# Cross-attention's keys and values by seven block products, made between self-attention's steps and handed on through DRAM

## The chip, the cores and the metric

The kernel runs on one core of a Trainium2 chip, with no work on the other cores. The metric is the device time of one execution in microseconds; the comparison uses the median of several executions. Its engines are called here by these names: PE is TensorE (matrix products and transposes, with results in PSUM), PEld is its weight load, DVE is VectorE, ACT is ScalarE, POOL is GpSimd and SP is SyncE, which issues most of the transfers between DRAM and SBUF. Each engine works through its own queue in order.

## The reference

One layer of a decoder in f32, on 8 sequences of 256 tokens with 1024 features, followed by a memory block and a last normalization:

```python
x = _layernorm(x + attn(x))              # 32 heads of 32, 8 key heads, causal
x = _layernorm(x + xattn(x, ctx))        # 32 heads of 128, 8 key heads
...                                      # memory block, sum, last normalization

# in xattn:
q = (query @ Wq).reshape(nb, q_len, H, D).transpose(0, 2, 1, 3)
k = (key @ Wk).reshape(nb, q_len, KVH, D).transpose(0, 2, 1, 3)
v = (value @ Wv).reshape(nb, q_len, KVH, D).transpose(0, 2, 1, 3)
q = q * cos + _rotate_half(q) * sin
k = k * cos + _rotate_half(k) * sin
k = jnp.repeat(k, GROUPS, axis=1)
v = jnp.repeat(v, GROUPS, axis=1)
scores = jnp.einsum('bhqd,bhkd->bhqk', q, k) / jnp.sqrt(jnp.float32(D))
scores = jnp.where(mask == 0, jnp.float32(-1000000000.0), scores)
attn = jax.nn.softmax(scores, axis=-1)
x = jnp.einsum('bhqk,bhkd->bhqd', attn, v)
return x.transpose(0, 2, 1, 3).reshape(nb, q_len, H * D) @ Wo
```

`key` and `value` are both the context `ctx`, 8 x 256 x 1024. Nothing in the keys and values of cross-attention depends on self-attention. The positions, and so the tables of cosines and sines, come from an input and are the same for queries and keys.

## The kernel before

Self-attention and cross-attention run one after the other.

**Self-attention** (L137 to L465) is a loop over 64 steps `s`, eight for each sequence `b`; step `c` of a sequence handles four heads. In a step TensorE transposes the four attention tiles (`transposed`, L280), does some other work (`others`, L357), projects the query of step s + 3 (`query`, L231), forms the weighted sum (`weighted`, L292) and makes the scores of step s + 2 (`scores`, L238). The other work is an output projection of the last sequence (`project_out`, L321) where c < 4, and a projection of the next sequence's keys or values where c is 4 or more; in steps 5 and 6 the normalized rows of the last sequence are also turned and written to DRAM for cross-attention (`turn`, L340). `scores` issues eight maxima on VectorE (L262), eight exponentials on ScalarE (L267) and four scalings on GpSimd (L274). The copy of a transposed tile out of PSUM (L289) is on VectorE for heads 0 and 2, on ScalarE for heads 1 and 3. The rotation of a projected query (`rope`, L200) takes a copy on ScalarE, one product on GpSimd (L202) and three operations on VectorE, the last of which (L207) needs GpSimd's product.

**Seven products.** Cross-attention's queries and output projection are already formed by a scheme with seven block products in place of eight: `xa_query` (L590) splits a pair of query heads, 256 output columns, and a quarter of the tokens, 512, into 2 x 2 blocks and adds the seven products `p1` to `p7` up in PSUM copies. It needs sums of weight blocks, made once: `sum_queries` and `sum_outputs` (L382, L397) load two weight tiles, combine them by four operations on GpSimd (`combine`, L380) and write the results to DRAM. Thirty-two of these sums are spread over self-attention's steps. It also needs sums of the input's blocks, T1 to T4, which `load_x1T` (L484) makes for each quarter.

**Cross-attention** (L834) runs over four quarters of 512 tokens (two sequences each) and 32 heads `H`; four heads share a key head `G`. While head H is transposed and weighted, the scores of head H + 1 are made. Between them stand the query parts, the output parts of the last group, and the next group's keys and values. These are plain products: `xa_keys` (L566) multiplies 8 tiles of weights with the context, 512 tokens wide, in one PSUM bank, and rotates the result; `xa_values` (L571) multiplies each 128-token chunk of the context with the value weights, 128 wide. The keys and values of a group live in SBUF, two of each. The last group of a quarter also loads the next quarter's context, positions and mask, and turns its tables (`xa_tables`, L538). Where there is room, `next_fill` (L828) puts in parts of the memory block.

**What sets the order.** TensorE's order is the program's order, by hand (L92). On the other engines the planner of the framework places the instructions by readiness, and of those that are ready the one earlier in the program first; it also assigns the buffers. A pool with n buffers makes the allocation n + 1 wait for a release. Weights of all kinds, and the turned rows, share seven buffers `w4` (L101) and are loaded by SP. PSUM has eight banks: in self-attention two `mm`, two `tr` and four for scores; in cross-attention four `mm`, two `tr`, two for scores. All transposes go through `tr`. `self.xa_early` (L469) loads quarter 0's inputs four steps before the end of self-attention, into space that self-attention's keys, values and inputs have freed.

Of the kernel before, what the change touches and what calls it, by code (L numbers as in the profile page):

```python
# [29 lines left out]
SA_STEPS = B * KC  # L30

# [10 lines left out]
W4 = 7  # L42
# [5 lines left out]
@with_exitstack  # L48
def decoder_layer(ctx: ExitStack, tc: tile.TileContext, a, out: bass.AP):

    Layer(ctx, tc, a, out).run()


class Layer:
    def __init__(self, ctx, tc, a, out):
# [5 lines left out]
        self.p_mm = [self.pool("mm", 2, space=PSUM)]  # L74
        self.turns = 0
        self.p_tr = self.pool("tr", 2, space=PSUM)
# [6 lines left out]
    def run(self):  # L83
# [7 lines left out]
        self.bias = self.const.tile([P, NB * 2, S], F32, name="bias")  # L91
# [17 lines left out]
    def tr(self):  # L109
        return self.p_tr.tile([P, 512], F32, name="tr")  # L110
# [26 lines left out]
    def self_attention(self):  # L137
# [50 lines left out]
        def project(lhs, xT):  # L188
# [7 lines left out]
            raw = uni.tile([P, S], F32, name="raw", bufs=2)  # L196
# [3 lines left out]
        def rope(dst, raw):  # L200
# [3 lines left out]
            t2 = uni.tile([P, S], F32, name="t2", bufs=2)  # L204
# [6 lines left out]
        def keys(b, i):  # L211
            if i == 0:
                kTs[b] = uni.tile([P, 2, S], F32, name="kT", bufs=2)
                vs[b] = uni.tile([P, 2, SA_KV * SA_D], F32, name="v", bufs=2)
            rope(kTs[b][:, i, :], project(wk[:, :, i * P : (i + 1) * P], xTs[b]))
# [15 lines left out]
        def query(s):  # L231
# [3 lines left out]
            qTs[s] = uni.tile([P, S], F32, name="qT", bufs=3)  # L235
            rope(qTs[s], raw)

        def scores(s):  # L238
# [15 lines left out]
            for sc in scs:  # L254
                att = sp.tile([P, 2, 384], F32, name="att", bufs=6)
# [24 lines left out]
        def transposed(s, j):  # L280
# [7 lines left out]
            at = sp.tile([P, 384], F32, name="at", bufs=6)  # L288
# [24 lines left out]
        def load_out(b, half):  # L313
            cols = slice(half * 512, (half + 1) * 512)
            wos[b, half] = []
            for c in range(0, KC, 2):
                w = sp.tile([P, 2, 512], F32, name="sa_wo", bufs=5)
# [22 lines left out]
        def turn(b, tt):  # L340
# [3 lines left out]
            for j in range(2):  # L344
                ps = self.tr()
# [11 lines left out]
        def others(s):  # L357
# [13 lines left out]
            elif c > 4:  # L371
                parts.append([lambda: self.xa_tables(0), lambda: self.xa_keys(0), lambda: self.xa_values(0, range(QT))][c - 5])
# [4 lines left out]
        self.query_sums, self.out_sums = {}, {}  # L377

# [3 lines left out]
        def sum_queries(m):  # L382

            wa = self.weights([P, KC, XA_D], a["xa_wq"][2 * m])
            wb = self.weights([P, KC, XA_D], a["xa_wq"][2 * m + 1])
            a11, a12, a21, a22 = wa[:, :4, :], wa[:, 4:, :], wb[:, :4, :], wb[:, 4:, :]
            combine(ALU.add, a22, a21, a22)
            combine(ALU.subtract, a21, a11, a21)
            combine(ALU.subtract, a11, a22, a11)
            combine(ALU.subtract, a12, a12, a11)  # L390
            self.query_sums[m] = []
            for i, w in enumerate((wa, wb)):
                d = self.dram.tile([P, KC, XA_D], F32, name=f"qs{i}_{m}")
                nc.gpsimd.dma_start(out=d, in_=w)
                self.query_sums[m].append(d)

        def sum_outputs(g, u):  # L397

            if u == 0:
                self.out_sums[g] = [self.dram.tile([P, 2, 512], F32, name=f"ot{i}_{g}") for i in range(4)]  # L400
            wa = self.weights([P, 2, 512], a["xa_wo"][GRP * g + u].rearrange("p (k c) -> p k c", k=2))
            wb = self.weights([P, 2, 512], a["xa_wo"][GRP * g + 2 + u].rearrange("p (k c) -> p k c", k=2))
            b11, b12, b21, b22 = wa[:, 0, :], wa[:, 1, :], wb[:, 0, :], wb[:, 1, :]
            combine(ALU.subtract, b11, b12, b11)
            combine(ALU.subtract, b12, b22, b12)
            combine(ALU.subtract, b22, b22, b11)
            combine(ALU.subtract, b21, b21, b22)
            for i, w in enumerate((b11, b22, b12, b21)):
                nc.gpsimd.dma_start(out=self.out_sums[g][i][:, u, :], in_=w)

        sums = [lambda m=m: sum_queries(m) for m in range(QP)]
        sums += [lambda g=g, u=u: sum_outputs(g, u) for g in range(XA_KV) for u in range(2)]

# [15 lines left out]
        for s in range(last):  # L429
# [9 lines left out]
            if s + 3 < last:  # L439
                query(s + 3)  # L440
# [871 lines left out]
```

## Time and profile before

| What | Value |
|---|---|
| Median of 3 executions | 3740.25 us (3739.35 to 3741.8) |
| The profiled execution | 3738.25 us, span of the profile 3736.5 us |
| Mean granted clock of TensorE | 0.978 |
| Busy shares | PE 96%, PEld 68%, DVE 50%, ACT 25%, POOL 25% |
| Moved by DMA | 494.39 MB, mean 132 GB/s |
| Chain that ended last | PE 87%, POOL 4%, DMA 3% |
| L600, query products, 128x256, x3584 | 841.5 us busy, 380 ns each |
| L561, keys, 128x512, x512 | 225.0 us busy, 592 ns each |
| L580, values, 128x128, x2048 | 238.8 us busy, 275 ns each |
| L380, sums of weights on POOL, x128 | 164.9 us busy |

A busy time of a group is the union of its instructions; the mean of one instruction includes the time that it takes to drain, so it is longer than the distance from one start to the next. The 40 slices are equal parts of the span, 93.4 us each; a digit is the busy share in tenths, and in the row of the clock the granted clock in tenths. Self-attention lies in the first ten slices, its last weighted sum ends at 926.83 us.

| Stretch | PE busy | DVE busy | POOL busy | granted clock | GB/s |
|---|---|---|---|---|---|
| 20 to 60 us | 31.32 of 40 | 16.99 | 18.48 | 0.88 | 266 |
| 240 to 400 us | 142.40 of 160 | 73.32 | 93.73 | 0.95 | 200 |
| 400 to 600 us | 180.78 of 200 | 100.23 | 120.64 | 0.96 | 206 |
| 600 to 800 us | 176.54 of 200 | 101.90 | 115.30 | 0.96 | 181 |
| 1100 to 1700 us | 599.51 of 600 | 306.91 | 101.59 | 1.00 | 117 |
| 3000 to 3600 us | 597.70 of 600 | 303.31 | 89.90 | 1.00 | 106 |

### The profile page before, as it was taken

Reading aid. Unit: us, or ns where it says so; the run is one execution under the profiler, and the core shown is the slowest. Engines: PE = TensorE matmul, PEld = TensorE weight load, DVE = VectorE, ACT = ScalarE, POOL = GpSimd, SP = SyncE. Lnnn points to the kernel's source line nnn. Section 1 sums busy time; section 2 is a strip of 40 time slices with the busy share of each in tenths; the row PEclk is TensorE's granted clock in tenths of the full one; section 3 lists DMA queues with packets and bytes.
Section 4 is the critical chain, followed back from the end, with each engine's and each line's share of the span. In section 5 each row is a group of like instructions: output and inputs, shape, how many; then the busy total and the mean of one; then the engine's idle time right before and its main releaser. Section 6 shows DMA issues by size and latency. Waiting matters only on the chain.

```text
span 3736.5 us, 47734 instructions
## 1 busy us (share of the span) xinstructions
PE 3595.0 (96%) x17294; PEld 2559.4 (68%) x17294; DVE 1851.0 (50%) x5574; ACT 942.0 (25%) x2920; POOL 933.9 (25%) x971
## 2 busy tenths in 40 slices
PE   7889988898999999999999999999999999999997
PEld 5656655665777777677777777777777777777764
DVE  3445544545444444564444555544455464444467
ACT  2333433333122212212121221222222121222213
POOL 4565556663111111121111111111112121111110
PEclk8999999999999999999999999999999999999996
DMA  6365555555433333433233343333334332333323
GB/s 229 119 241 179 198 180 191 203 202 173 150 99 108 107 104 110 161 122 107 94 109 103 105 158 102 126 106 102 99 103 152 113 121 98 101 103 105 103 81 129
DMA packets 182298, 494.39 MB, mean 132 GB/s; under 512 B 17072, under 2 KB 45040, under 8 KB 180144
## 3 DMA queue, kind: packets, MB, share of 16 engines
q1 hardware_dynamic: 142592, 406.73, 32.9%
q0 software_dynamic: 15104, 52.44, 3.8%
q10 hardware_dynamic: 24368, 32.18, 2.3%
q8 instruction: 138, 2.26, 0.3%
q14 instruction: 96, 0.79, 0.1%
HBM read 425.88 MB, written 65.40 MB: 131 GB/s over the span
## 4 chain that ended last, share of the span: by engine, by line
PE 87%; POOL 4%; DMA 3%; ACT 2%; DVE 2%; issue 1%; SPq 0%; POOLq 0%; DVEq 0%; ACTq 0%
PE mm L600 21%; PE mm L764 20%; PE mm L580 6%; PE mm L192 6%; PE sc L665 6%; PE mm L561 6%; PE mm L715 6%; PE mm L329 4%; PE tr L699 3%; POOL w L380 2%; ACT att L267 2%; PE tr L284 2%; PE mm L1013 2%; PE mm L1149 1%; DMA w<-in_xa_wq 1%
## 5 line engine op out<-in xcount | busy, mean ns | idle before, releaser
L600 PE MATMUL mm<-x1T,w 128*128 128x256 f32 x3584 | 841.5, 380 | 3.2 <-DVE res L771 3.2
L600 PEld LDWEIGHTS mm<-x1T,w 128*128 128x128 f32 x3584 | 668.7, 190 | 129.0 <-issue 44.8
L556 POOL TENSOR_TENSOR qT<-qT,t 128x512 f32<-128x512 f32 x128 | 162.3, 1268 | 1334.2 <-DVE t L555 1161.8
L764 PE MATMUL mm<-w,xoS 128*128 128x512 f32 x992 | 446.2, 592 | 1.4 <-DVE t L555 1.4
L679 ACT ACTIVATE xatt<-xatt,nmax 128x256 f32<-128x256 f32 x512 | 255.7, 500 | 691.9 <-DVE nmax L674 679.1
L764 PE MATMUL mm<-w,xoT 128*128 128x512 f32 x744 | 334.4, 592 | 0.0
L764 PEld LDWEIGHTS mm<-w,xoS 128*128 128x128 f32 x992 | 188.2, 190 | 186.8 <-issue 172.7
L267 ACT ACTIVATE att<-att,nmax 128x128 f32<-128x128 f32 (+1 forms) x512 | 225.4, 442 | 249.0 <-DVE nmax L262 249.0
L771 DVE TENSOR_TENSOR acc<-mm,acc 128x512 f32<-128x512 f32 x216 | 148.5, 689 | 275.2 <-PE mm L764 275.1
L665 PE MATMUL sc<-kT,qT 128*128 128x256 f32 x1024 | 263.7, 381 | 0.0
L192 PE MATMUL mm<-xT,w 128*128 128x256 f32 x1024 | 258.4, 410 | 0.0
L607 DVE TENSOR_TENSOR raw<-mm,half 128x256 f32<-128x256 f32 x256 | 107.8, 421 | 298.7 <-PE mm L600 298.6
L274 POOL TENSOR_TENSOR att<-att,rec 128x256 f32<-128x256 f32 (+1 forms) x256 | 205.9, 827 | 156.0 <-DVE rec L271 149.6
L715 PE MATMUL mm<-xat,v 128*128 128x256 f32 x1024 | 243.3, 380 | 0.9 <-ACT xat L704 0.9
L580 PEld LDWEIGHTS mm<-w,ctxT 128*128 128x128 f32 x2048 | 238.5, 192 | 3.2
L580 PE MATMUL mm<-w,ctxT 128*128 128x128 f32 x2048 | 238.8, 275 | 0.0
L764 PEld LDWEIGHTS mm<-w,xoT 128*128 128x128 f32 x744 | 141.4, 190 | 138.7 <-issue 114.6
L192 PEld LDWEIGHTS mm<-xT,w 128*128 128x128 f32 x1024 | 210.1, 211 | 31.3
L730 POOL TENSOR_TENSOR xoS<-xoT 128x512 f32<-128x512 f32 x62 | 78.5, 1265 | 603.9 <-ACT xoT L724 603.9
L561 PE MATMUL mm<-ctxT,w 128*128 128x512 f32 x512 | 225.0, 592 | 1.4 <-DMA w<-in_xa_wk 1.4
L329 PE MATMUL mm<-sa_wo,sa_oT 128*128 128x512 f32 x512 | 225.0, 592 | 0.0
L771 DVE TENSOR_TENSOR res<-mm,res 128x512 f32<-128x512 f32 x186 | 127.9, 687 | 193.2 <-PE mm L764 170.8
(187 smaller groups left out, 4710.5 us busy)
## 6 DMA issues: line engine op xcount, KB each, us to landing
w<-in_xa_wo SPq DMA_DIRECT2D x129, 512.0 KB, 3.8
w<-qs SPq DMA_DIRECT2D x128, 512.0 KB, 3.3
w<-ot SPq DMA_DIRECT2D x124, 512.0 KB, 3.3
w<-in_xa_wq SPq DMA_DIRECT2D x96, 512.0 KB, 3.5
w<-in_sa_wq SPq DMA_DIRECT2D x64, 512.0 KB, 5.6
sa_wo<-in_sa_wo SPq DMA_DIRECT2D x64, 512.0 KB, 4.6
qs<-w POOLq DMA_DIRECT2D x32, 512.0 KB, 4.0
ot<-w POOLq DMA_DIRECT2D x64, 256.0 KB, 4.0
```

Source lines behind the costliest of these rows:

```text
L192: nc.tensor.matmul(ps[:, :S], lhsT=lhs[:, k, :], rhs=xT[:, k, :], start=(k == 0), stop=(k == KC - 1),)
L267: nc.scalar.activation(att[:, jj, lo:hi], att[:, jj, lo:hi], AF.Exp, bias=nmax[:, i : i + 1], scale=-1.0, accum_out=sums[:, i : i + 1],)
L274: nc.gpsimd.tensor_tensor(att[:, :, lo:hi], att[:, :, lo:hi], rec[:, :, i : i + 1].to_broadcast([P, 2, hi - lo]), ALU.mult,)
L329: nc.tensor.matmul(ps, lhsT=oTs[b * KC + c][:, tt * P : (tt + 1) * P], rhs=wos[b, half][c // 2][:, c % 2, :], start=(c == 0), stop=(c == K ...
L561: self.nc.tensor.matmul(ps, lhsT=w[:, k, :], rhs=rhs(k), start=(k == 0), stop=(k == KC - 1))
L580: nc.tensor.matmul(ps[:, tt * P : (tt + 1) * P], lhsT=self.ctxT[:, k, tt * P : (tt + 1) * P], rhs=self.wv[:, k, :], start=(k == 0), stop=( ...
L600: nc.tensor.matmul(ps[:, :S], lhsT=lhs[:, k, :], rhs=self.xb[q][rhs][:, k, :], start=(k == 0), stop=(k == 3),)
L665: nc.tensor.matmul(sc[:, qt, :], lhsT=qT[:, q0 : q0 + P], rhs=kT[:, b * S : (b + 1) * S], start=True, stop=True,)
L679: nc.scalar.activation(att[:, qt, :], att[:, qt, :], AF.Exp, bias=nmax[:, qt : qt + 1], scale=-1.0, accum_out=sums[:, qt : qt + 1],)
L715: nc.tensor.matmul(po[:, b * S : (b + 1) * S], lhsT=self.v[G][:, NB * b + kt, :], rhs=at[:, kt * S : (kt + 1) * S], start=(kt == 0), stop= ...
L764: nc.tensor.matmul(ps, lhsT=oT[lhs][:, u, off + p * P : off + (p + 1) * P], rhs=w[:, u, :], start=(u == 0), stop=(u == 1),)
L771: nc.vector.tensor_tensor(dst, ps, dst, ALU.add)
```

## The change

- `xa_query`'s seven products become a function `seven` for any pair of weights. Cross-attention's keys and values go through it too (`xa_keys_values`): for each quarter and pair of key heads seven products for the keys, 256 wide, and seven for the values in a turned form, where the context is the stationary operand and the weights move, 128 wide.
- These 224 products, four per step, are made in self-attention's steps 4 to 59. Rotated keys, values and the tables of each quarter go to DRAM and are loaded by cross-attention, keys and values one group ahead.
- The context is loaded in blocks with their sums, once per quarter, in self-attention (`xa_context`). The weights of keys and values get their own sums, eight more; every sum is loaded in one step and combined in the next.
- Self-attention's step is reordered: scores of step s + 1 first, then the transposes one at a time with products, the query of s + 2 and the other work between them. Scores are now one step ahead, queries two.
- Buffers: weights nine instead of seven; attention and transposed tiles of self-attention four instead of six; its output weights four instead of five. PSUM: three `mm` and one `tr` in self-attention, four and two in cross-attention. Several tiles of self-attention move from a shared pool to its own.
- In cross-attention the keys and values go away, the two blocks of a head are transposed one at a time with a query part between, and filler has two places per head.

```diff
-W4 = 7
+W4 = 9
+KV_BEGIN, KV_END = 4, 60
...
-        self.p_mm = [self.pool("mm", 2, space=PSUM)]
-        self.p_tr = self.pool("tr", 2, space=PSUM)
+        self.p_mm = [self.pool("mm", 3, space=PSUM)] * 3
+        self.p_tr = [self.pool("tr", 1, space=PSUM)]
...
-                att = sp.tile([P, 2, 384], F32, name="att", bufs=6)
+                att = sp.tile([P, 2, 384], F32, name="att", bufs=4)
-            at = sp.tile([P, 384], F32, name="at", bufs=6)
+            at = sp.tile([P, 384], F32, name="at", bufs=4)
-                w = sp.tile([P, 2, 512], F32, name="sa_wo", bufs=5)
+                w = sp.tile([P, 2, 512], F32, name="sa_wo", bufs=4)
...
+        def sums_of_inputs(name, m):
+            wa = self.weights([P, KC, XA_D], a[name][2 * m])
+            wb = self.weights([P, KC, XA_D], a[name][2 * m + 1])
+            def run():
...
+            return run
...
+        sums = [lambda n=n, m=m: sums_of_inputs(n, m) for m in range(XA_KV // 2) for n in ("xa_wk", "xa_wv")]
+        sums += [lambda m=m: sums_of_inputs("xa_wq", m) for m in range(QP)]
+        sums += [lambda g=g, u=u: sums_of_outputs(g, u) for g in range(XA_KV) for u in range(2)]
...
+        products = [part for q in range(NQ) for m in range(XA_KV // 2) for part in self.xa_keys_values(q, m)]
...
-            ats = [transposed(s, 0), transposed(s, 1)]
-            for part in others(s):
-                part()
-            ats += [transposed(s, 2), transposed(s, 3)]
-            if s + 3 < last:
-                query(s + 3)
-            if s >= 3 and (s - 3) * len(sums) // 56 < (s - 2) * len(sums) // 56 <= len(sums):
-                sums[(s - 3) * len(sums) // 56]()
-            weighted(s, ats)
-            if s + 2 < last:
-                scores(s + 2)
+            done = later
+            later = begins[s]() if s in begins else None
+            n = NQ * XA_KV // 2 * 14 // (KV_END - KV_BEGIN)
...
+            first = (s - KV_BEGIN) * n % (XA_KV // 2 * 14) == 0
...
+            if s + 1 < last:
+                scores(s + 1)
+            ats = [transposed(s, 0)]
+            if not first:
+                one()
+            ats.append(transposed(s, 1))
+            if not first:
+                one()
+            if done:
+                done()
+            ats.append(transposed(s, 2))
+            if s + 2 < last:
+                query(s + 2)
+            ats.append(transposed(s, 3))
+            for part in others(s):
+                part()
+            weighted(s, ats)
+            while mine:
+                one()
...
+    def seven(self, name, m, xb, turned, done):
...
+        def product(w, block):
+            ps = self.mm()
+            rhs = xb()[block]
+            if turned:
+                for t in range(2):
+                    for k in range(4):
+                        nc.tensor.matmul(
+                            ps[:, t * P : (t + 1) * P], lhsT=rhs[:, k, t * P : (t + 1) * P], rhs=w[:, k, :],
+                            start=(k == 0), stop=(k == 3),
+                        )
+            else:
+                for k in range(4):
+                    nc.tensor.matmul(
+                        ps[:, :S], lhsT=w[:, k, :], rhs=rhs[:, k, :], start=(k == 0), stop=(k == 3)
+                    )
...
+    def xa_keys_values(self, q, m):
+        def keys(i, c):
+            G = q * XA_KV + 2 * m + i
+            kT = self.hp.tile([P, TQ], F32, name="kx", bufs=2)
+            self.xa_rope(kT, c)
+            self.kT_d[G] = self.dram.tile([P, TQ], F32, name=f"kT_{G}")
+            nc.gpsimd.dma_start(out=self.kT_d[G], in_=kT)
+        def values(i, c):
...
+            nc.gpsimd.dma_start(out=self.v_d[G], in_=c.rearrange("p (t d) -> p t d", d=XA_D))
...
             for i, dst in enumerate((self.cos, self.sin)):
-                nc.vector.tensor_copy(dst[:, tt * P : (tt + 1) * P], ps[:, i * P : (i + 1) * P])
+                (nc.scalar.copy if i else nc.vector.tensor_copy)(
+                    dst[:, tt * P : (tt + 1) * P], ps[:, i * P : (i + 1) * P]
+                )
+        self.tables_d[q] = self.dram.tile([P, 2, TQ], F32, name=f"tables_{q}")
...
             out()
-            self.xa_transposed(H)
+            self.xa_transposed(H, 0)
             if not waits:
                 query()
...
-            elif i == 0:
-                self.xa_keys(G + 1)
-            else:
-                self.xa_values(G + 1, range(2 * i - 2, 2 * i))
+            self.xa_transposed(H, 1)
...
+            self.next_fill()
             self.xa_weighted(H)
```

## The prediction

> **What bounds the kernel now.** I read the busy shares and the 40 slices first, then TensorE's own waits, then two stretches of the timeline.
>
> ```profile
> PE   7889988898999999999999999999999999999997
> DVE  3445544545444444564444555544455464444467
> PEclk8999999999999999999999999999999999999996
> ```
>
> TensorE is full from the eleventh slice on (93.4 us each) and not before it. Self-attention fills the first ten slices. No other engine comes near full. So in cross-attention only fewer or cheaper TensorE instructions help; in self-attention it is the waits.
>
> How much is lost there? In the timeline a step without a gap, from the scores at 510.60 us to those at 524.04, takes 13.44 us, 6.87 of it an output projection (16 matmuls); the bare step is 6.57, and a key or value projection adds 3.46. The 64 bare steps (420.5), 28 output projections (192.4), 28 projections for the next sequence (96.9), 14 turns at 0.95 (13.3), quarter 0's tables, keys and values (1.0 + 6.97 + 7.14), less 12.3 done before the loop, plus 25.9 in front of it, make 752 us. From the first projection at 10.51 to the last weighted sum at 926.83 are 916.3 us. So **164 us are lost**, 28 of them up to the end of step 3 at 91.14, where four bare steps take 51.6.
>
> ```profile
> PE tr L284 <- DVE at L289: 61.8, 17, 9.7
> PE tr L284 <- ACT at L289: 21.4, 32, 0.9
> ...
> DVE qT L207 <- POOL t L202: 79.3, 17, 12.1
> ...
> POOL w L380 <- DMA w<-in_xa_wo: 18.1, 10, 5.0
> POOL w L380 <- DMA w<-in_xa_wq: 17.1, 6, 8.1
> ```
>
> These are lines of the waits (total, times, longest): TensorE's over the whole run, the others in 100 to 900 us. TensorE waits at the attention's transposes for their PSUM bank. The rotation of queries waits on GpSimd, which stands in line at weight sums whose operands have not landed. One step shows the first wait:
>
> ```profile
> 432.69 0.94 PE L247 MATMUL sc<-kT,qT 32*128 32x128 f32 x16
> 433.55 0.88 PE L284 MATMUL tr<-ident,att 128*128 128x128 f32 x6
> 434.02 0.28 DVE L262 CUSTOM_DVE_ANT_0 att<-sc,mask 128x128 f32<-128x128 f32 x1
> 436.34 0.53 DVE L289 COPY at<-tr 128x384 f32<-128x384 f32 x1
> 437.87 0.46 ACT L289 COPY at<-tr 128x384 f32<-128x384 f32 x1
> ```
>
> The transposes are over at 434.4, yet VectorE copies the first one only at 436.34, behind all eight max operations of the scores that stand earlier in the program; ScalarE copies the second behind all eight exponentials. From the first max operation the copies end after 2.85 and 4.3 us. The step from 457.49 and that from 510.60 show the same distances.
>
> **The products: 55 us saved.**
>
> ```profile
> 1302.58 3.60 PE L764 MATMUL mm<-w,xoS 128*128 128x512 f32 x8
> 1306.01 1.04 PE L699 MATMUL tr<-ident,xatt 128*128 128x128 f32 x8
> 1306.88 1.89 PE L600 MATMUL mm<-x1T,w 128*128 128x256 f32 x8
> 1308.61 3.73 PE L580 MATMUL mm<-w,ctxT 128*128 128x128 f32 x32
> 1312.18 1.89 PE L715 MATMUL mm<-xat,v 128*128 128x256 f32 x8
> ```
>
> Start to start (each busy time holds a drain that overlaps the next line): eight instructions 512 wide take 3.43 us, eight 256 wide 1.73, 32 of 128 wide 3.57. One matmul in the code is two instructions here. Now: keys 32 x 6.87 = 219.8, values 64 x 3.57 = 228.5, together 448.3. After: four quarters, four pairs of heads, seven products make 112 for keys at 1.73 = 193.8, and 112 for values (two column halves, four chunks each, 128 wide) at 1.785 = 199.9, together 393.7. Saved: **54.6**.
>
> A rule speaks against this. The Trainium skill, "TensorE: Matmul & The Clock Gate", section "Back-to-back issue gap", gives streams of loads and matmuls 81 ns at width 128 and 131 ns at 512: narrow matmuls cost more per column. A line through both gives about 98 ns at 256, 1.5 times the price per column, so keys would cost 7/8 x 219.8 x 1.5 = 288 instead of 194 and the saving would become a loss of 40. The rows show 0.429 us at 512 and 0.216 at 256, the same per column within 1%, for these f32 tiles. I take the rows.
>
> **What self-attention loses afterwards: 146 us.** Four products per step, 7 us, stand in steps 4 to 59. A step becomes 20.4 us (output projection) or 17.0 (others) of TensorE work. The softmax chain, which now holds short steps at 12 to 13, is then covered. But the transposes keep one bank instead of two. With the scores at time 0, they end at 0.86, the first transpose at 1.22, a product at 2.95. The second transpose needs the copy of the first: VectorE starts on the max operations at about 1.1 (in cross-attention, 1.07 after the scores' start at 1320.80) and the copy ends at 3.95, TensorE goes on at 4.1. That is 1.15 us, and I take 1.35, because the last product's addition (0.42) or a key rotation (2.06) can stand ahead. The third transpose, at 6.2 or later, finds ScalarE's copy done (5.4). Bounds: 0 where the copy slips ahead of the max operations, 2.9 where a rotation always stands ahead. In the sum:
> - 48 plain steps: 65.
> - Four steps in which a new quarter's context begins, with no product between transposes: 2.8 + 0.9 = 3.7 each, 15.
> - Start and steps 0 to 3, as now less a little: 28.
> - Last four steps, two without products, and the first block loads behind the freed space: 16 (8 to 30).
> - Tables: eight transposes per quarter, between the first transpose and its copy, sharing its bank: 3 each, 12 (4 to 25).
> - Differences of the context blocks (three VectorE operations of 2.06 per quarter) and late weights: 10 (0 to 40).
>
> So the waits change from 164 to 146: **18 us** come back. Gaps near 1 us leave the clock alone: 513 to 526 us, with none, was granted 1.00; 474 to 487, around a gap of 3.3, 0.75.
>
> **Edits that I cost at nothing, and their cover.**
> - VectorE: 14 additions at 0.42 per pair, 94 us, beside 66 of rotations that move along. It was busy 450 of the first 950 us and stays near half; TensorE's products cover it. Uncovered, it delays the copies above.
> - GpSimd: eight more sums (32 operations of 1.29, 16 stores of 0.57: 50 us), 31 more rotation adds (39), 64 stores of keys and values (36), three more block differences and 12 gathers (19). 520 us in the first 950, issues included, become 665 of some 1290. A store of values waits for VectorE's addition, and the scaling of attention and the queries' first rotation product stand behind it: at most 0.42 each, against 6 us between that product and the scores that need it.
> - Sums are loaded one step before they are combined, 17 us against 3.8 to landing. That removes GpSimd's 35 us at L380; what then comes last is the bank above.
> - SP's queue: 172 MB in 20 to 950 us become 275, 215 GB/s; 436 to 448 us ran at 325. Stores of tables wait for their copies with weight loads behind them; nine slots, with some five loads per step, give more than a step of lead. Four output weight tiles instead of five: the next half's loads wait for a projection, a step ahead of their use, against 4.6 us to land.
> - Renamed tiles issue nothing. Four attention tiles suffice, as the scores now come one step ahead at the step's start instead of two at its end.
> - Cross-attention loads keys and values (256 KB each) three heads before use. Its bank counts stay. Without filler, the weighted sum follows the second transpose at once: ScalarE's copy comes out 0.25 + 0.53 later, the first block's matmuls cover 0.86. I take 0.1 for some 90 heads, **10 us** (0 to 40). Filler twice per head has work enough between dependent parts.
>
> **Sum:** 3738.25 - 54.6 - 18 + 10 = 3675 against the profiled execution (span 3736.5). The median is 2 us above it: **3677**.
>
> **Rivals.**
> 1. *The bank wait is hidden* (copies run early): 65 us go, 3612. For it: a planner places VectorE's work. Against: in every step that I looked at the copy came behind the eight. Chance 0.22.
> 2. *GpSimd's queue still stands at the sums*: slower. Now 17 rotations wait for it, and around 480.68 it costs TensorE a 3.3 us gap and a query projection at half clock (5.8 for 3.6), 5.5 together. Sums rise from 32 to 40, and their loads wait for slots that earlier sums hold; SP already shows that:
>
> ```profile
> SPq L102 <- DMA ot<-w: 109.4, 28, 12.4
> SPq L102 <- DMA qs<-w: 97.7, 23, 7.6
> ```
>
> With 14 such steps left of the present 17 the time is 3677 + 77 = 3754; it decides from 12 on. Against: the load has a step's lead. Chance 0.17, and 0.06 for a few such steps, near no change.
> 3. *The forecast*: the bank wait replaces the others, 3677, chance 0.55.
>
> That the products don't fall to seven eighths is excluded by the code's counts.
>
> **Numbers.** Case 1 and the forecast are faster: 0.77. A change within 0.2% (7.5 us, about what can be told from none) has 0.06, slower 0.17. The range runs from case 1 to case 2, 3605 to 3755; the forecast's own is 3640 to 3715.
>
> **What would show it.** 896 key instructions 256 wide at 0.216 and 1792 of values 128 wide at 0.112 start to start; self-attention ending near 1290 us; TensorE's largest wait at the attention's transposes for VectorE's copy, about 50 times 1.3 us; no half-clock slices between 100 and 1200; L380's wait for loads near zero. I am wrong if products are spaced wider than 1.8 us, if that wait is missing or above 2.5 us per step, or if cross-attention shows repeated gaps before its weighted sums.

## The result, and the profile after

The changed kernel takes 3784.26 us (median of four executions, 3781.02 to 3785.28), the kernel before 3741.03 beside it: 1.0114 times as long, 95% interval 1.0097 to 1.0132. The profiled execution has a span of 3779.2 us and a mean granted clock of 0.970 (before: 3736.5 and 0.978). It is slower, where faster was forecast.

First the busy rows and slices of the changed kernel's page:

```profile
PE 3583.5 (95%) x17422; PEld 2614.6 (69%) x17422; DVE 2013.4 (53%) x5794; ACT 943.1 (25%) x2905; POOL 1036.0 (27%) x1087
...
PE   5899999899999979999999999999999999999997
...
DVE  3445445444446444455566565556465566465556
...
PEclk8899999999999989999999999999999999999996
```

A slice is 94.5 us. Self-attention's last weighted sum ends at 1387.9 us, in the fifteenth slice; 1290 was predicted. Up to there the rows of TensorE and of its clock still have digits below 9, and a 9 can hide a loss of some per cent. The remaining 2391 us are nearly full, as before. So most of the miss lies in self-attention. TensorE's waits over the whole run (total, times, longest) say where:

```profile
PE tr L287 <- DVE at L292: 80.2, 57, 4.8
PE sc L250 <- DVE sa_qT L210: 13.7, 7, 8.3
PE mm L647 <- DMA w<-in_xa_wq: 12.3, 2, 12.1
PE tr L609 <- DVE at L292: 9.1, 4, 2.3
PE tr L287 <- ACT at L292: 8.1, 10, 1.0
PE tr L287 <- POOL att L277: 6.5, 3, 5.2
```

The first line is the wait that the prediction named, 57 times; "about 50 times 1.3 us" is right in place and number, and on average (1.41) nearly in size. But the average hides two kinds of step, which the timeline separates. Here are rows of TensorE, and in the second step of VectorE too (start, duration, engine, line, operation; in brackets the idle time before it and what ended it):

```profile
1263.21 0.94 PE L250 MATMUL sc<-sa_kT,sa_qT 32*128 32x128 f32 x16
...
1264.46 1.89 PE L647 MATMUL mm<-ctxT,w 128*128 128x256 f32 x8
1267.14 0.55 PE L287 MATMUL tr<-ident,att 128*128 128x128 f32 x3 [0.79 <-DVE at L292]
...
1284.77 0.94 PE L250 MATMUL sc<-sa_kT,sa_qT 32*128 32x128 f32 x16
1285.34 0.69 DVE L622 TENSOR_TENSOR kx<-raw,cos 128x512 f32<-128x512 f32 x1
...
1286.74 0.69 DVE L625 TENSOR_TENSOR t<-raw,sin 64x512 f32<-64x512 f32 x1
1287.45 0.29 DVE L265 CUSTOM_DVE_ANT_0 att<-sc,mask 128x128 f32<-128x128 f32 x1
...
1289.84 0.53 DVE L292 COPY at<-tr 128x384 f32<-128x384 f32 x1
1290.42 0.90 PE L287 MATMUL tr<-ident,att 128*128 128x128 f32 x3 [2.50 <-DVE at L292]
1291.11 3.08 PE L641 MATMUL mm<-w,ctxT 128*128 128x128 f32 x16
```

In the first step the second transpose waits 0.79 us for the copy behind eight maxima. In the second step a key rotation (L622 to L625) stands in front of the maxima too: the step's last product before the scores was the sixth of a seven, whose addition lets the rotation go. The wait is 2.50 us, and the product after it takes 3.08 us instead of the 1.95 of the same product in experiment 9: TensorE runs at half clock for a while. This wait comes in every seventh step, eight times; a slow stretch follows seven of the eight.

Adding up steps against their bare work, as the prediction did, gives this (us lost of the 1377.8 from the first projection to the last weighted sum):

| Part of self-attention | predicted | measured |
|---|---|---|
| up to the fifth step's scores (113.5 us) | 28 | 55 |
| 40 plain steps without a rotation ahead | 54 of the 65 | 63.7 |
| 8 plain steps with one | 11 of the 65 | 36.1 |
| late weights, block differences | 10 | in the two rows above |
| 4 steps in which a context begins | 15 | 29.4 |
| 4 steps with tables | 12 | 22.5 |
| last four steps | 16 | 29 |
| **Sum** | **146** | **236** |

The last row leaves out 6.9 us for four of cross-attention's query products, which now stand ahead of the last weighted sum: they are work that moved, not a loss. Of the 236 us TensorE stands idle for 149 (it is busy for 1228.94 of the 1377.8). The other 87 pass while it is busy, a good part of them at half clock; before the change the two were 104 and 60.

Behind self-attention the border to cross-attention became 12 us shorter, but by work that left it: three query products, and an output projection that now stands behind the first cross-attention scores. Cross-attention itself, from its first scores to the end, takes 2370.6 us. It was 2776.9; less the 437 of products and table transposes that left it, and with the 5 that came over the border, it should take 2345: 26 us lost instead of 10.

### The profile page after: what moved, and what is told of

The parts are those of the page before. It is cut to its first block, busy times and chain, and to the rows that moved or that the text cites. A ratio compares the mean times of both kernels' runs of the same rounds, so it can differ in the third digit from the quotient of the medians.

```text
span 3779.2 us, 48961 instructions
## 1 busy us (share of the span) xinstructions
PE 3583.5 (95%) x17422; PEld 2614.6 (69%) x17422; DVE 2013.4 (53%) x5794; ACT 943.1 (25%) x2905; POOL 1036.0 (27%) x1087
## 4 chain that ended last, share of the span: by engine, by line
PE 81%; DVE 8%; POOL 4%; DMA 3%; issue 2%; ACT 2%; SPq 0%; POOLq 0%; ACTq 0%; DVEq 0%
PE mm L647 22%; PE mm L844 18%; PE mm L195 6%; PE mm L795 6%; PE sc L746 5%; PE mm L332 5%; PE mm L641 4%; DVE att L265 3%; PE tr L779 3%; PE tr L287 2%; PE mm L1079 2%; POOL w L379 1%; PE mm L1219 1%; ACT att L270 1%; PE sc L250 1%
## 5 line engine op out<-in xcount | busy, mean ns | idle before, releaser
L653 DVE TENSOR_TENSOR raw<-mm,half 128x256 f32<-128x256 f32 x384 | 161.7, 421 | 317.3 <-PE mm L647 271.9
L653 DVE TENSOR_TENSOR half<-mm,half 128x256 f32<-128x256 f32 x288 | 121.3, 421 | 296.6 <-PE mm L647 250.1
L795 PE MATMUL mm<-xat,v 128*128 128x256 f32 x1024 | 255.8, 390 | 5.7 <-ACT xat L784 5.7
L784 ACT COPY xat<-tr 128x512 f32<-128x512 f32 x256 | 148.9, 586 | 411.6 <-PE tr L779 411.6
L287 PE MATMUL tr<-ident,att 128*128 128x128 f32 x768 | 142.5, 297 | 98.8 <-DVE at L292 80.2
L641 PE MATMUL mm<-w,ctxT 128*128 128x128 f32 x1792 | 227.9, 285 | 5.8 <-DVE res L337 4.9
L641 PEld LDWEIGHTS mm<-w,ctxT 128*128 128x128 f32 x1792 | 218.2, 200 | 11.4 <-DVE res L337 5.3
```

The lines of the kernel that those rows point to most:

```text
L287: nc.tensor.transpose(pt[:, i * P : (i + 1) * P], atts[s][j // 2][:, j % 2, i * P : (i + 1) * P], self.ident,)
L641: nc.tensor.matmul(ps[:, t * P : (t + 1) * P], lhsT=rhs[:, k, t * P : (t + 1) * P], rhs=w[:, k, :], start=(k == 0), stop=(k == 3),)
L653: nc.vector.tensor_tensor(out, in0, in1, ALU.add)
L795: nc.tensor.matmul(po[:, b * S : (b + 1) * S], lhsT=self.v[G][:, NB * b + kt, :], rhs=at[:, kt * S : (kt + 1) * S], start=(kt == 0), stop= ...
```

## The experiments

All of them start from the changed kernel (3784). The time before, run beside them, was 3741.7 to 3744.1.

**1. The order of scores and transposes.** The scores of step s + 1 move from the front of the step to behind its second transpose.

```diff
-            if s + 1 < last:
-                scores(s + 1)
             ats = [transposed(s, 0)]
             ...
             ats.append(transposed(s, 1))
+            if s + 1 < last:
+                scores(s + 1)
```

> The scores of step s + 1 are issued after the second transpose instead of before the first; nothing else changes. Theory A (a transposed tile's copy stands in VectorE's queue behind the eight maxima of the scores issued before it, and the single bank makes TensorE wait for it): TensorE's waits at the attention's transposes for VectorE's copy fall from 80 us to below 25, the waits of 2.5 us every seventh step and the half clock after them go, and the time falls by 45 to 65 us from 3784, to 3720 to 3740. Theory B (the softmax of the scores, now one step ahead, is too slow for the step, and the bank is only where it shows): the waits come back at the scalings or at the next transposes, and the time stays within 15 us of 3784.

Measured: 3709.06 us (3706.26 to 3710.6), 0.9904 [0.9888, 0.9921] of before: 75 us less than the changed kernel, more than theory A expected (45 to 65), although the waits for the copy did not fall below 25 us as it said; theory B is excluded. TensorE's waits of this kernel:

```profile
PE tr L287 <- DVE at L292: 35.8, 21, 4.1
PE tr L287 <- POOL att L277: 15.5, 6, 12.9
...
PE mm L641 <- DVE res L337: 10.7, 3, 5.3
```

From one step's scores to the next, the 40 plain steps lose 39.2 us instead of 63.7, the eight with a rotation 22.6 instead of 36.1, those with a context's beginning or tables together 31 instead of 52; the start to the fifth step's scores takes 106.4 us instead of 113.5. The maxima cannot stand before the first copy when their scores do not exist yet. Some of the gain is given back: products now wait for their own banks (the third line).

**2. A second bank for transposes.** Two banks for products and two for transposes in self-attention, as before the change.

```diff
-        self.p_mm = [self.pool("mm", 3, space=PSUM)] * 3
-        self.p_tr = [self.pool("tr", 1, space=PSUM)]
+        self.p_mm = [self.pool("mm", 2, space=PSUM)]
+        self.p_tr = [self.pool("tr", 2, space=PSUM)]
...
-        self.p_mm.append(self.pool("xa_mm", 1, space=PSUM))
-        self.p_tr.append(self.pool("xa_tr", 1, space=PSUM))
+        self.p_mm.append(self.pool("xa_mm", 2, space=PSUM))
```

> Two banks for transposes and two for products in self-attention instead of one and three, the order as in the changed kernel. If the number of banks for transposes decides: the waits for VectorE's copy fall from 80 us to below 25 and the time by 40 to 60 us, to 3725 to 3745. If the copy's place in VectorE's queue decides, whatever the banks: products now wait for their two banks, whose additions stand in the same queue, and less than 20 us is gained.

Measured: 3716.27 us (3713.28 to 3728.7), 0.9924 [0.9907, 0.994]: 68 us less, again more than expected. The waits for VectorE's copy fall from 80.2 to 25.5 us:

```profile
PE tr L287 <- DVE at L292: 25.5, 16, 4.7
```

So the number of banks and the order in the queue are two cures of one wait, and either alone is worth some 70 us.

**3. No sums for the key and value weights.** The 32 GpSimd combinations of these weights are left out (the loads and stores stay).

```diff
             def run():
                 a11, a12, a21, a22 = ...
-                combine(ALU.add, a22, a21, a22)
-                ...
+                if name == "xa_wq":
+                    combine(ALU.add, a22, a21, a22)
+                    ...
```

> Leaves out the 32 combinations on GpSimd for the key and value weights (the loads and stores stay), most of which fall into steps 0 to 7. If GpSimd's queue is what lengthens the start: the start of step 4 moves from 113.5 us back to 85 to 95, and the time falls by 18 to 30 us, to 3754 to 3766. If the start waits for the loads of the context and of weights: step 4 starts within 5 us of 113.5, and the time stays within 6 us.

Measured: 3767.7 us (3760.72 to 3771.99), 1.0061 [1.0044, 1.0078]: 17 us less; the fifth step's scores stand at 105.8 us instead of 113.5. Both numbers fall between the two expectations. GpSimd's work is part of the slow start, not the whole of it. (In runs 4 to 7, which do not touch the start, the same scores stand at 115.9 to 116.6 us; differences in the start are good to about 3 us.)

**4. Cross-attention's order.** Both blocks of a head are transposed at once, the query part comes between them and the weighted sum.

```diff
             self.xa_transposed(H, 0)
+            self.xa_transposed(H, 1)
             if not waits:
                 query()
-            self.xa_transposed(H, 1)
```

> In cross-attention both blocks of a head are transposed at once and the query part stands between them and the weighted sum, as before the change. If the weighted sum waits for ScalarE's copy of the second block: the weighted sums' busy time falls from 255.8 to about 244 us, their named wait from 5.7 to below 1, and the time by 12 to 20 us, to 3764 to 3772. If cross-attention loses its 17 us elsewhere: within 4 us of 3784.

Measured: 3772.18 us (3769.5 to 3776.86), 1.008 [1.0063, 1.0097]: 12 us less. The busy time of the weighted sums falls from 255.8 to 245.2 us, about as expected, but the wait that the profile names does not fall (6.0 us against 5.7): the gain is inside a group. TensorE's rows of one head, in the changed kernel:

```profile
1929.21 0.60 PE L779 MATMUL tr<-ident,xatt 128*128 128x128 f32 x4
1929.64 2.02 PE L795 MATMUL mm<-xat,v 128*128 128x256 f32 x8
1931.51 3.60 PE L844 MATMUL mm<-w,xoS 128*128 128x512 f32 x8
```

and in this experiment:

```profile
1925.33 1.89 PE L647 MATMUL mm<-x1T,w 128*128 128x256 f32 x8
1927.06 1.89 PE L795 MATMUL mm<-xat,v 128*128 128x256 f32 x8
1928.79 1.45 PE L844 MATMUL mm<-w,xoS 128*128 128x512 f32 x3
```

From the weighted sum's start to the next line are 1.87 us in the first and 1.73 in the second. The second half of the group waits 0.14 us for ScalarE's copy without an idle time of its own in the list. In the changed kernel 88 of the 128 heads have transposes directly ahead of the weighted sum, in this run 6: 82 x 0.14 = 11.5, about the gain measured.

**5. The rotation one product later.** The first key head's rotation is issued ahead of the seventh product instead of behind the sixth.

```diff
         def p3():
             add(now["c1"][:, S:], ps, now["u2"])
-            done(0, now["c1"])
+            if turned or name != "xa_wk":
+                done(0, now["c1"])
 
         def p4():
+            if not turned and name == "xa_wk":
+                done(0, now["c1"])
             w = self.weights([P, 4, XA_D], self.a[name][2 * m + 1][:, 4:, :])
```

> Changed kernel with the first key head's rotation of a pair put one product later, ahead of the seventh product instead of behind the sixth. Every seventh step then no longer begins with that rotation ahead of the eight maxima. Theory: the rotation's three VectorE operations (2.06 us) ahead of the maxima make the second transpose wait 2.5 us in eight steps, and the half clock that follows costs as much again: 4.4 us of loss becomes about 1.2 to 1.5, so 20 to 26 us go, about 3760; TensorE's waits at the transposes for VectorE's copy fall from 80 to about 65 us. Rival: the copy is late for the eight maxima alone and the clock drops for another reason, then the same steps still lose over 3 us and the time stays within 6 us of 3784.

Measured: 3785.55 us (3780.02 to 3795.02), no change, and the same eight steps wait 2.5 us as before. The trace shows why this is no answer to the question: at 1282.68 us the rotation is again ahead of the maxima, at 1284.80. VectorE's order is the planner's, by readiness; the rotation's operand is there before the scores, so its place in the program does not matter.

**6. The eighth product back.** The second block product of each seven is added twice into its bank, so that its share counts double: 16 key and 16 value products more, 56 us of work.

```diff
...
-            ps = product(now["a"][:, 4:, :], "B21")
+            ps = product(now["a"][:, 4:, :], "B21", 1 if name == "xa_wq" else 2)
```

> Changed kernel with the second block product of each seven taken twice (added twice into its bank, so that keys and values differ): eight products' work again instead of seven, 16 pairs with one key product (1.73) and one value product (1.785) more, 56 us. Theory: the saving is whole in place, TensorE is the bound between the transposes too, and at most 6 us of it vanish in waits for a late copy: 3834 to 3842. Rival: part of the saving was never on the path, because TensorE waits after a product anyway; then the extra products cost under 35 us and the time is below 3820.

Measured: 3830.8 us (3824.09 to 3835.89), 1.0231 [1.021, 1.0253]: 46.5 more than the changed kernel, between the two expectations and nearer the first. So 83% of an eighth product's work appears in the time. Some 10 us do not; at least part of them is taken from waits, as TensorE waits for VectorE's copy 51 times instead of 57. The saving of seven against eight exists, and in this place it is worth about 46 us, not 56.

**7. No query products in the last two steps.** Their weights were waited for 12.1 us, because their load stands behind loads for which space was still held.

```diff
-            elif s > last - 3:
-                mine, self.queries = self.queries[:2], self.queries[2:]
```

> Changed kernel without cross-attention's query products in self-attention's last two steps; all seven then stand behind the loop, where they stood in part before. Theory: their weights are asked for behind four block loads that wait for the last query's freed space, TensorE waits 12.1 us for them and then works at half clock; 6 to 12 us go, about 3774, and the last weighted sum comes nearer to the scores before it. Rival: the same load is then waited for behind the loop instead, because nothing asks for it earlier, and the time stays within 4 us of 3784.

Measured: 3783.92 us (3781.59 to 3785.92), no change: the rival's number, but by another wait than it named. VectorE and TensorE of this kernel:

```profile
1362.09 0.08 DVE L265 DVE_READ_ACCUMULATOR2_ANT nmax<- 128x1 f32 x1
1366.01 1.23 DVE L544 TENSOR_TENSOR x1T<-x1T 128x1024 f32<-128x1024 f32 x1 [3.84 <-DMA x1T<-x1T]
...
1367.24 0.53 DVE L292 COPY at<-tr 128x384 f32<-128x384 f32 x1
...
1367.82 0.90 PE L287 MATMUL tr<-ident,att 128*128 128x128 f32 x3 [7.52 <-DVE at L292]
```

VectorE stands at the first block difference of x1T, whose load has not landed, with the copy that TensorE needs behind it. The late load costs the same through another door; the loads of x1T wait for the space that the last query's projection frees (24.6 us in SP's queue in the changed kernel, 24.5 here), and the query weights are loaded behind them.

**8. GpSimd's order by hand.** GpSimd keeps the program's order throughout, as TensorE does.

```diff
-        with self.tc.manual_schedule(engines={PE}):
+        with self.tc.manual_schedule(engines={PE, mybir.EngineType.Pool}):
```

> Changed kernel with GpSimd's order also kept as written instead of placed by readiness. Theory: at the start the planner puts weight sums and the gathers of the context's tables ahead of the queries' first rotation product; kept as written, the scalings and that product come first and the start to the fifth step's scores falls from 113.5 us to about 100, 8 to 14 us less in all unless later steps lose by it. Rival: the order on GpSimd matters little at the start, because the bare steps wait for the softmax chain anyway: the fifth step begins within 4 us of 113.5; and stores that wait for their operands then stand ahead of scalings, so the time is 3784 or above.

Measured: 3823.62 us (3821.58 to 3826.45), 1.0217 [1.02, 1.0234]. The theory's start holds: the fifth step's scores are at 100.0 us, 13.5 earlier. GpSimd of the changed kernel,

```profile
44.90 1.56 POOL L379 TENSOR_TENSOR w<-w 128x512 f32<-128x512 f32 x1
...
47.37 3.17 POOL L277 TENSOR_TENSOR att<-att,rec 128x256 f32<-128x256 f32 x4
50.51 2.34 POOL L548 TENSOR_TENSOR ctxT<-ctxT 128x1024 f32<-128x1024 f32 x1
...
66.61 0.73 POOL L205 TENSOR_TENSOR t<-sa_raw,sa_cos 128x256 f32<-128x256 f32 x1
```

and with the order by hand:

```profile
33.14 6.05 POOL L277 TENSOR_TENSOR att<-att,rec 128x256 f32<-128x256 f32 x4 [3.38 <-DVE rec L274]
...
49.46 0.73 POOL L205 TENSOR_TENSOR t<-sa_raw,sa_cos 128x256 f32<-128x256 f32 x1 [5.40 <-ACT sa_raw L200]
```

The first scaling of attention comes 14 us earlier and the fifth rotation product 17 us earlier, because sums, gathers and block differences no longer stand ahead of them. But half of the gain is gone by the end of self-attention (first cross-attention scores at 1401.3 us against 1408.6), and cross-attention loses 48 us, with longer waits of TensorE for ScalarE's copies (20.4 us against 5.7) and for GpSimd's rotations (13.5 against 1.0). A fixed order helps where it is right and costs wherever it is not.

**9. Without the rotation.** One in four key heads stays unrotated: those whose rotation is the last thing before the scores. This is the test that run 5 did not make.

```diff
-            self.xa_rope(kT, c)
+            if i == 0 and m % 2:
+                nc.scalar.copy(kT, c)
+            else:
+                self.xa_rope(kT, c)
```

> Changed kernel with one in four of the key heads left unrotated (a ScalarE copy in its place): the first head of the second and fourth pair of each quarter, whose rotation is the last thing before the scores in eight of the 56 steps. Theory: those eight steps lose 1.2 us like the others instead of 2.8 to 6.5, so 22 to 30 us go and the time is 3754 to 3762. Rival: the second transpose waits in those steps for something else than the rotation; then the time stays within 8 us of 3784 and the steps keep their waits of 2.5 us.

Measured: 3757.59 us (3753.24 to 3765.25), 1.004 [1.0029, 1.005]: 27 us less, inside the theory's span. The same step as above, now:

```profile
1264.62 0.94 PE L250 MATMUL sc<-sa_kT,sa_qT 32*128 32x128 f32 x16
...
1265.59 0.29 DVE L265 CUSTOM_DVE_ANT_0 att<-sc,mask 128x128 f32<-128x128 f32 x1 [0.44 <-PE sc L250]
...
1267.97 0.53 DVE L292 COPY at<-tr 128x384 f32<-128x384 f32 x1
...
1268.56 0.55 PE L287 MATMUL tr<-ident,att 128*128 128x128 f32 x3 [0.80 <-DVE at L292]
1268.94 1.95 PE L641 MATMUL mm<-w,ctxT 128*128 128x128 f32 x16
```

The maxima start 0.97 us after the scores instead of 2.68, the wait is 0.80, and the product runs at full clock. The eight steps lose 10.8 us in place of 36.1, which is 25 of the 27 us.

**10 to 12. Versions put together.** Run 10 has the edits of runs 1 and 4.

> Changed kernel with the scores behind the second transpose, and cross-attention's two blocks of a head transposed before the query part. Theory: the two gains (75 and 12 us alone) lie in different stages and add up: 3693 to 3702. Rival: cross-attention's gain alone came from the border between the stages, which the first edit moves: about 3709, as with the first edit alone.

Measured: 3696.54 us (3694.61 to 3697.5), 0.987 [0.9854, 0.9886] of before. The gains add up (75 + 12 = 87, measured 88), and this version beats both kernels: 46 us faster than before. Run 11 adds GpSimd's order by hand, in self-attention alone:

```diff
-        with self.tc.manual_schedule(engines={PE}):
+        with self.tc.manual_schedule(engines={PE, mybir.EngineType.Pool}):
             self.self_attention()
+        with self.tc.manual_schedule(engines={PE}):
             self.cross_attention()
```

> The kernel with both orders changed, and GpSimd's order as written during self-attention alone (by readiness in cross-attention again). Theory: by hand the start was 13.5 us shorter and cross-attention 47 us longer; with the order kept to self-attention the start's gain stays in part, 7 to 12 us: 3683 to 3694. Rival: the start was latency of the bare steps, which the scores behind the second transpose already change, and stores in line ahead of scalings cost as much later: within 4 us of the kernel without this edit.

Measured: 3727.26 us (3723.56 to 3730.63), 31 us more than run 10, outside both expectations. The fifth step begins at 98.1 us instead of 106.7, and everything is lost again behind it. VectorE's largest wait between the start and the end of self-attention in run 10, and below it the same line of run 11:

```profile
DVE sa_qT L210 <- POOL t L205: 134.1, 36, 13.6
```

```profile
DVE sa_qT L211 <- POOL t L206: 247.1, 45, 10.2
```

With the order fixed, the query's rotation waits longer for its product on GpSimd, where sums and stores can stand ahead that are not ready, and VectorE's later copies stand behind that rotation. This is a reading of the waits; no run takes it apart.

Run 12 adds to run 11 the banks of run 2.

> As the last one, with two banks for transposes and two for products in self-attention. Theory: the scores behind the second transpose leave some 36 us of waits for VectorE's copy, which a second bank takes away, while two product banks give back 20 to 38 us of waits at products, as in the run with two banks alone: 3680 to 3705, no clear gain. Rival: the waits at products overlap those that stay anyway, then 3665 to 3680.

Measured: 3782.5 us (3780.3 to 3786.96), 55 us more than run 11, outside both expectations as well, though the same edit alone brought 68. TensorE's largest waits from 115 to 1380 us:

```profile
PE mm L647 <- DVE res L338: 30.1, 10, 7.2
PE mm L641 <- DVE sa_oT L311: 19.9, 6, 5.2
PE mm L641 <- DVE res L338: 15.6, 9, 3.2
PE mm L641 <- DVE w L353: 14.8, 3, 6.6
```

No wait for VectorE's copy at the attention's transposes is left there; every one of these lines is a product that waits for VectorE to empty one of two banks. With the scores moved and GpSimd's order by hand, the third product bank is worth more than the second transpose bank. Whether that holds for run 10, without the order by hand, was not tried.

## Why the prediction was wrong

The step that failed is "**What self-attention loses afterwards: 146 us**". It lost 236, and the change gave nothing back there: 72 us more than the 164 before, where 18 less were forecast. These 72, less the 55 saved, plus the 26 of cross-attention, are the 43 us by which the kernel is slower. Point by point:

- **Products, "Saved: 54.6"**: right in the rates (key products follow each other at 1.73 us, value products at 1.78). The rule on narrow matmuls that the prediction weighed there, with its estimate of 98 ns at width 256, does not hold here: it is 0.216 us at 256 and 0.112 at 128, the same per column within 4%. In place an eighth product of work, 56, is worth 46 (run 6).
- **"48 plain steps: 65"**: the mechanism is right, and for 40 of the 48 the size too (63.7, with the 10 for late weights in it). The mis-sized term is "**I take 1.35, because the last product's addition (0.42) or a key rotation (2.06) can stand ahead**". The rotation was spread as a small mean over all steps. It stands ahead in eight steps, whole, and there lifts the wait from 0.8 to 2.5 us: 36 us lost instead of 11. Run 9 takes it away and 27 us go.
- **"Gaps near 1 us leave the clock alone"**: the two stretches named beside it, one without a gap and one around a gap of 3.3 us, do not show this, but the changed kernel does (a step with a gap of 0.79 us was granted 1.00, in the last section). The conclusion "no half-clock slices between 100 and 1200" failed: gaps of 2.5 us came, and seven of the eight were followed by a stretch at half clock. The sum has no term for that; six of those seven steps lose 4.4 to 4.6 us each, nearly twice their gap.
- **"Start and steps 0 to 3, as now less a little: 28"**: 55. The change moves loads, sums, gathers and block differences into just those steps, and the planner put them ahead of the attention's scalings and the query's rotation. The prediction counted GpSimd's work as a total ("520 us ... become 665") with at most 0.42 us for what stands behind a store, and no place where it is dense. Run 8, with GpSimd in program order, starts 13.5 us sooner; run 3, without the sums, 7.7. The other half of the 27 us is not separated; the bare steps, whose scores come one step ahead instead of two, were not tried with another distance.
- **"Four steps in which a new quarter's context begins ... 15" and "Tables ... 12"**: 29.4 and 22.5. The waits alone were not far off: 3.5 to 5.4 us in a step of the former, where 3.7 were forecast, and about 2.3 in a step of the latter, where 3 were. But slow products follow (the steps from 413.19 and 440.16 us were granted 0.87 and 0.88), and the sum again has nothing for them. No run isolates the two.
- **"Last four steps ... 16"**: 29, without the query products. Run 7 shows that the late block loads set the largest wait there, 12.1 us, whichever instruction meets them first.
- **"10 us" for cross-attention**: the mechanism and its size were right (0.14 us for 82 heads, run 4). Some 15 us more were lost there. About 10 of these lie between 1420 and 1480 us, where TensorE idles 5.8 us, 4.3 of them for the memory block's weights, and the clock is 0.91; why those weights come late was not tried.
- **"That removes GpSimd's 35 us at L380"**, and the sign that this wait would be near zero, failed: from 100 to 1388 us GpSimd waits 79 us for the loads of sums (L379 in the changed kernel). TensorE feels little of it directly, as the next point shows; why the loads land so late was not tried. The two largest lines:

```profile
POOL w L379 <- DMA w<-in_xa_wo: 47.5, 8, 10.3
...
POOL w L379 <- DMA w<-in_xa_wq: 24.1, 8, 5.1
```

- **Rival 2**, the slower one, put the blame on GpSimd's queue in 14 steps throughout. That wait (scores for the rotated query) totals 13.7 us, 12.9 of them before 120 us: it decided the start alone. **Rival 1**, copies that slip ahead of the maxima, did not happen by the planner, but run 1 made it happen by the program: 75 us, where 65 were estimated for it.

Of the 107 us between forecast and result, 90 are self-attention's and 16 cross-attention's. The start (27) and the steps with a rotation (25) are the largest terms of the 90. Run 9 shows the cause of the second; of the first, runs 3 and 8 show a part each. Run 1 shows the largest single cause of what self-attention loses, forecast or not: what stands in VectorE's queue ahead of the one copy that frees the only transpose bank. It is the bank wait that the forecast named, priced with too good a queue and without the clock that follows a long wait.

## What to carry to other kernels

When a change leaves one buffer between two engines, list what can stand in the emptying engine's queue ahead of the copy, step by step and with its period, and price the worst step whole: a mean over steps hides that a gap of 2.5 us can cost nearly twice its length, by the clock. Work that is hidden "beside" something must be placed, not totalled: the queue on GpSimd that holds up the scores costs TensorE 12.9 us before 120 us and 0.8 after. And two edits that each cure the same wait need not add up: a second transpose bank brought 68 us alone, and cost 55 on top of run 11, where the copy was early already.

## What the runs showed of the hardware that was not expected

- The clock: the Trainium skill, "TensorE: Matmul & The Clock Gate", section "What's actually happening", has the half rate come after an idle window of about 3.4 us. Here gaps of 2.45 to 2.51 us were enough in seven of eight steps, and once not; nor was the gap of 2.78 us that ends at 793.60. What counts is where the gap falls. In all fourteen traces of this case every stretch at half clock that ends inside the trace lasts 3.41 us or a multiple of it, and all of one trace begin on one grid of that spacing. Call a piece between two points of the grid a cell. From 160 to 1380 us of each trace, a cell at full clock in which TensorE was busy for 1.4 us or less was always followed by half clock, and one with 1.8 us or more never; between these both occur. So a gap of 2.5 us trips the clock when nearly all of it lies in one cell, and need not when it is split over two. Below are the plain step and the stretch behind the gap of 2.50 us, then a cell that tripped the clock with the one after it, and one that did not, again with the one after it (bounds, length, busy times of the five engines, TensorE first, granted clock, DMA share, GB/s):

```profile
1263.20:1284.70 21.50, 20.71 (x109) 13.99 (x108) 8.64 (x32) 4.78 (x19) 3.95 (x5) 1.00 0.44 139
...
1290.40:1296.00 5.60, 5.58 (x30) 5.40 (x31) 4.13 (x6) 1.86 (x8) 4.82 (x5) 0.73 0.35 121
...
528.89:532.30 3.41, 1.17 (x11) 1.17 (x12) 3.38 (x17) 3.41 (x17) 3.39 (x5) 1.00 0.90 331
532.30:535.71 3.41, 3.41 (x17) 3.23 (x16) 3.37 (x4) 0.61 (x2) 3.41 (x4) 0.50 0.80 298
...
791.71:795.13 3.42, 1.53 (x14) 1.53 (x15) 2.35 (x14) 3.30 (x15) 2.82 (x3) 1.00 0.54 206
795.13:798.54 3.41, 3.41 (x23) 3.13 (x22) 0.89 (x2) 0.00 (x0) 3.37 (x6) 1.00 0.35 107
```

- A VectorE product of two SBUF tiles, L209, took 3.37 us at 59.84 us, beside GpSimd's scalings and sums, and 0.43 at 23.34 beside none. "SBUF — State Buffer", section "Who interferes with whom", says that a VectorE instruction with two SBUF inputs contends with GpSimd's reads. The trace agrees, and not at the start alone: the 80 executions of L209 take 0.41 to 3.37 us, 0.57 at the median, and the ten that ran beside no GpSimd arithmetic at most 0.45.
- A wait inside a group of matmuls need not appear as idle time: experiment 4's 11.5 us stand in no list of waits, only in the distance between two starts.
